# Layer 0 of a two-layer transformer: the FFN's, preparation's and output's matmuls queued behind the scores

## The chip, the cores and the metric

The kernel runs on one core of a Trainium2 chip. The metric is the device time of one launch in microseconds. Five engines with queues of their own work side by side: TensorE (matmuls and transposes, PE in the profile, its weight loads PEld), VectorE (DVE), ScalarE (ACT), GpSimd (POOL) and SyncE (SP, which here issues transfers).

## The reference, cut to what matters

Sixteen sequences of 512 tokens of width 128 run through two layers. The change touches layer 0 alone: half an FFN with FP4 quantization, attention with relative positions in keys and values, and half of the same FFN again.

```python
# layer 0, per sequence x [512, 128]; ln = layernorm without weights
def ffn(x):   # I = 352
    q = fp4_quant_dequant            # blocks of 16: scale = max|x|/6, values rounded to 8 steps
    h = silu(q(x) @ q(w_gate).T) * (q(x) @ q(w_up).T)
    return q(h) @ q(w_down).T
def attn(x):  # 16 heads of 8
    q, k, v = split(x @ W_qkv + b_qkv); q = q / sqrt(8)
    score = q k^T + q . rel_emb_k[clip(j - i, -64, 64) + 64]
    p = softmax(score)
    ctx = p v + p . rel_emb_v[clip(j - i, -64, 64) + 64]
    return ctx @ W_out + b_out
x = x + 0.5 * ffn(ln(x))
x = x + attn(ln(x))
x = x + 0.5 * ffn(ln(x))
# layer 1 follows (attention with experts, linear attention, attention with experts)
```

## The kernel before

The unit of work in layer 0 is half a sequence of queries (256 rows, all 16 heads); 32 units make the 16 sequences. Each is passed twice. `maxima` computes the scores of a unit in 32 blocks of 128 x 512 (`scores`, L263 and L267: four matmuls, and eight more where relative positions vary), reduces each on VectorE (L341), and from these gets the row maxima: two reductions (L347), a transpose on TensorE (L349), and transfers that put the negated maximum into the score operand as a bias row (L353, L355). `main` computes the 32 blocks again, now with the bias; ScalarE takes the exponential (L369), and the products with the values (`av`) and with the relative values (`rps`) follow in runs of 16 to 64 matmuls (`run`, L272 and L274). Score blocks of both passes share three PSUM buffers (`sps`, pool `pS`).

Around this run chains of smaller steps, written as Python generators that yield between steps:

- `head` and `tail`: `F.half`, half an FFN over 256 rows. Layernorm (L55 to L62), quantization (L70 to L81, the last two on GpSimd), transposes (L115) and a copy (L116), two times gate and up (L121 to L126), quantization, and for each of two halves transposes (L133), copies (L135, L136), three matmuls (L139) and the addition (L140). `head` works three sequences ahead; `tail` ends a unit and stores it.
- `prep` and `prepV`: layernorm, transposes (L282), Q and K (L286), splitting into two float16 parts and transfers to memory in another layout, products with the relative keys (L305); V (L319, L321). `prep` works two sequences ahead.
- `fin`: the output of the unit before. The addition of the relative part (L422), transposes (L430), the division by the softmax sums (L433, L434), transposes (L437), a copy (L438), the product with W_out (L440), additions (L442, L443).

All these matmuls write to two PSUM buffers (`mps`, pool `pM`).

A planner, `interleave`, decides in which order the code emits all this: each generator has a number of steps and a span of due times in units, and the generator whose next step is due first is called next. From the emitted order and from what depends on what, the language's scheduler makes each engine's final queue. It may issue an instruction ahead of ones emitted before it, where by its own account it is ready sooner. `tc.issue_after(ins)` is a means against this: what is traced inside it stands behind `ins` in the queue of `ins`'s engine; it adds an order and no wait. Before the change it is used for the runs of `av` and `rps` matmuls (L273) and for the addition of `fin` on VectorE (L425). Once in the queue, an engine's instructions start in order: one that waits holds up those behind it.

Before the loop stands a start: the first sequence's head, its preparation, its first maxima, the heads and preparation of the second sequence, 14 steps of the next maxima, the heads of the third.

Of the kernel before, what the change touches and what calls it, by code (L numbers as in the profile page):

```python
# [17 lines left out]
I = 352  # L18
# [7 lines left out]
class K:  # L26
# [23 lines left out]
    def ln_steps(s, xb, out, wk, n):  # L50

        nc=s.nc
        st=wk.tile([128,n,6],F32,name="ln_st"); mv=wk.tile([128,n,2],F32,name="ln_mv")
        for j in range(n):
            nc.vector.bn_stats(st[:,j,:],xb[:,j,:])  # L55
            nc.vector.bn_aggr(mv[:,j,:],st[:,j,:]); yield  # L56
        ve=wk.tile([128,n],F32,name="ln_ve"); rs=wk.tile([128,n],F32,name="ln_rs"); mr=wk.tile([128,n],F32,name="ln_mr")
        nc.vector.tensor_scalar(ve,mv[:,:,1],1e-5,None,ALU.add)  # L58
        nc.gpsimd.tensor_tensor(rs,ve,s.negh[:,:n],ALU.pow); yield  # L59
        nc.vector.scalar_tensor_tensor(mr,mv[:,:,0],-1.0,rs,ALU.mult,ALU.mult)  # L60
        for j in range(n):
            nc.scalar.activation(out[:,j,:],xb[:,j,:],AF.Identity,bias=mr[:,j:j+1],scale=rs[:,j:j+1])  # L62
        yield
    def quant_steps(s, X, wk, P, nb, tag):

        nc=s.nc
        n=nb*16
        X3=X.rearrange("p (b k) -> p b k",k=16)
        sc=wk.tile([128,nb],F32,name=tag+"_sc"); ri=wk.tile([128,nb],F32,name=tag+"_ri")
        nc.vector.tensor_reduce(sc[:P],X3,axis=AX.X,op=ALU.max,apply_absolute_value=True)  # L70
        nc.vector.tensor_scalar(sc[:P],sc[:P],float(np.float32(1/6)),1e-12,ALU.mult,ALU.max)
        nc.vector.reciprocal(ri[:P],sc[:P]); yield
        y=wk.tile([128,max(704,n)],F32,name=("q_y","q_yw")[n>704])[:,:n]; y3=y.rearrange("p (b k) -> p b k",k=16)
        nc.vector.tensor_tensor(y3[:P],X3,ri[:P].unsqueeze(2).to_broadcast([P,nb,16]),ALU.mult); yield
        M=wk.tile([128,max(704,n)],F32,name=("q_M","q_Mw")[n>704])[:,:n]
        nc.vector.tensor_scalar(M[:P].bitcast(U32),y[:P].bitcast(U32),0x7F800000,None,ALU.bitwise_and)
        nc.vector.tensor_scalar(M[:P],M[:P],1.0,C_MAG,ALU.max,ALU.mult); yield
        nc.vector.scalar_tensor_tensor(y[:P],y[:P],SHRINK,M[:P],ALU.mult,ALU.add); yield  # L78
        nc.gpsimd.tensor_tensor(M[:P],y[:P],M[:P],ALU.subtract)  # L79
        M3=M.rearrange("p (b k) -> p b k",k=16)  # L80
        nc.gpsimd.tensor_tensor(M3[:P],M3[:P],sc[:P].unsqueeze(2).to_broadcast([P,nb,16]),ALU.mult)  # L81
        yield M

class FFN:
# [22 lines left out]
    def half(f, xb, half, wk, pp):  # L107

        s=f.s; nc=s.nc
        xh=xb[:,2*half:2*half+2,:]  # L110
        xn=wk.tile([128,2,128],F32,name="f_x")
        yield from s.ln_steps(xh,xn,wk,2)
        for xq in s.quant_steps(xn.rearrange("p a b -> p (a b)"),wk,128,16,"xq"): yield
        ps=pp.tile([128,512],F32,name="mps")
        for j in range(2): nc.tensor.transpose(ps[:,j*128:(j+1)*128],xq[:,j*128:(j+1)*128],s.ident)  # L115
        xqT=wk.tile([128,256],F32,name="f_x"); nc.scalar.copy(xqT,ps[:,:256]); yield  # L116
        h=wk.tile([128,2,I],F32,name="f_h")
        for j in range(2):
            t=h[:,j,:]
            g=pp.tile([128,512],F32,name="mps")  # L120
            nc.tensor.matmul(g[:,:I],xqT[:,j*128:(j+1)*128],f.wguT[:,0,:],start=True,stop=True)  # L121
            nc.scalar.activation(t,g[:,:I],AF.Tanh,scale=0.5)
            nc.vector.scalar_tensor_tensor(t,t,1.0,g[:,:I],ALU.add,ALU.mult); yield
            u=pp.tile([128,512],F32,name="mps")
            nc.tensor.matmul(u[:,:I],xqT[:,j*128:(j+1)*128],f.wguT[:,1,:],start=True,stop=True)
            nc.vector.scalar_tensor_tensor(t,u[:,:I],0.5,t,ALU.mult,ALU.mult); yield  # L126
        for hq in s.quant_steps(h.rearrange("p a b -> p (a b)"),wk,128,44,"hq"): yield
        hq=hq.rearrange("p (a b) -> p a b",a=2)
        for j in range(2):
            ps=pp.tile([128,512],F32,name="mps")  # L130
            for c in range(3):
                P=min(128,I-c*128)
                nc.tensor.transpose(ps[:P,c*128:(c+1)*128],hq[:,j,c*128:c*128+P],s.ident)  # L133
            hT=wk.tile([128,3,128],F32,name="hT",bufs=1)
            nc.scalar.copy(hT[:,0:2,:],ps[:,:256])  # L135
            nc.scalar.copy(hT[:96,2,:],ps[:96,256:384])  # L136
            for c in range(3):
                P=min(128,I-c*128)
                nc.tensor.matmul(ps[:,384:512],hT[:P,c,:],f.wdT[:P,c,:],start=(c==0),stop=(c==2),skip_group_check=True)  # L139
            nc.vector.scalar_tensor_tensor(xh[:,j,:],ps[:,384:512],0.5,xh[:,j,:],ALU.mult,ALU.add); yield  # L140

def f16split(nc, src, hi, lo, eng_lo):
# [3 lines left out]
class Attn0:  # L146
# [110 lines left out]
    def scores(a, out, kt, half, b, BD, TQ, KS):  # L257

        nc=a.nc; blk=half*8+b
        sd=a.side(kt,blk); ib=a.inband(kt,blk)  # L260
        o4=out.rearrange("p (x g c) -> p g x c",x=8,g=4)
        for g in range(4):
            nc.tensor.matmul(o4[:,g],KS[:,sd,g*512+kt*128:g*512+(kt+1)*128],BD[:,g,:,b*32:b*32+32].rearrange("p h (x j) -> p x h j",j=4),start=(g==0),stop=(not ib and g==3),skip_group_check=True)  # L263
        if ib:
            for x in range(8):
                w0=kt*128-blk*32-x+a.OFF
                nc.tensor.matmul(out[:,x*64:x*64+64],a.ET[:,w0:w0+128],TQ[:,:,b*32+4*x:b*32+4*x+4],start=False,stop=(x==7),skip_group_check=True)  # L267

    xnT={}; pend={}; last=None
    def run(a, mms):  # L270
# [4 lines left out]
    def prep(a, b, xb, wk, pM):  # L275
# [3 lines left out]
        xn=wk.tile([128,4,128],F32,name="xn")  # L279
        yield from s.ln_steps(xb,xn,wk,4)  # L280
        ps=pM.tile([128,512],F32,name="mps")
        for j in range(4): nc.tensor.transpose(ps[:,j*128:(j+1)*128],xn[:,j,:],a.ident)  # L282
        xnT=a.xnT[b]=wk.tile([128,512],F32,name="xnT",bufs=2); nc.scalar.copy(xnT,ps); yield
        for z in range(2):
            ps=pM.tile([128,512],F32,name="mps")
            nc.tensor.matmul(ps,a.w[:,z*128:(z+1)*128],xnT,start=True,stop=True)  # L286
            f=wk.tile([128,512],F32,name="qk0") if z==0 else wk.tile([128,4,128],F32,name="xn").rearrange("p a b -> p (a b)")
            if z==0:
                for hf in range(2):
# [12 lines left out]
                nc.sync.dma_start((QS,KSd)[z][:,p*8:p*8+8,:],t)  # L302
            yield
        ps=pM.tile([128,512],F32,name="mps")
        nc.tensor.matmul(ps[:32],a.eb.rearrange("p a b -> p (a b)"),q,start=True,stop=True)  # L305
        rhi=wk.tile([128,512],F16,name="qkhi",bufs=2)[:32]; rlo=wk.tile([128,512],F16,name="qklo")[:32]
        nc.vector.tensor_copy(rhi,ps[:32]); nc.vector.tensor_tensor(rlo,ps[:32],rhi,ALU.subtract)
        for sd in range(2):
# [23 lines left out]
    def maxima(a, b, half, wk, pS, pM):  # L332
# [12 lines left out]
        mk=wk.tile([128,2,8,8],F32,name="mk")  # L345
        for hh in range(2):
            nc.vector.tensor_reduce(mk[:,hh],mx.rearrange("p k (x s) b -> p s b x k",s=2)[:,hh],axis=AX.X,op=ALU.max)  # L347
        ps=pS.tile([128,512],F32,name="sps")
        nc.tensor.transpose(ps[:,:128],mk.rearrange("p s b x -> p (s b x)"),a.ident)  # L349
        mt=wk.tile([128,32],F32,name="mt"); mn=wk.tile([128,32],F16,name="mn")  # L350
        nc.vector.tensor_reduce(mt,ps[:,:128].rearrange("p (c q) -> p q c",c=4),axis=AX.X,op=ALU.max)
        nc.vector.tensor_scalar(mn,mt,-1.0,None,ALU.mult)
# [63 lines left out]
    def fin(a, b, half, X, wk, pM):  # L416
# [10 lines left out]
        cn=wk.tile([128,2,128],F32,name="cn")  # L427
        for t in range(2):
            ps=pM.tile([128,512],F32,name="mps")
            for z in range(4): nc.tensor.transpose(ps[:,z*128:z*128+128],cx[:,z,t*128:t*128+128],a.ident)  # L430
            p3=ps.rearrange("p (h c) -> p h c",c=32)
            rc=wk.tile([128,16],F32,name="rc")
            nc.vector.reciprocal(rc,p3[:,:,8])  # L433
            nc.vector.tensor_tensor(cn[:,t,:].rearrange("p (h d) -> p h d",d=8),p3[:,:,0:8],rc.unsqueeze(2).to_broadcast([128,16,8]),ALU.mult)  # L434
            yield
        ps=pM.tile([128,512],F32,name="mps")
        for t in range(2): nc.tensor.transpose(ps[:,t*128:t*128+128],cn[:,t,:],a.ident)  # L437
        ct=wk.tile([128,2,128],F32,name="cn").rearrange("p a b -> p (a b)"); nc.scalar.copy(ct,ps[:,:256])  # L438
        ps=pM.tile([128,512],F32,name="mps")
        for t in range(2): nc.tensor.matmul(ps[:,t*128:(t+1)*128],ct[:,t*128:(t+1)*128],a.wo,start=True,stop=True)  # L440
        xh=xb[:,2*half:2*half+2,:]
        nc.gpsimd.tensor_tensor(xh,xh,a.bo.unsqueeze(1).to_broadcast([128,2,128]),ALU.add)  # L442
        nc.vector.tensor_tensor(xh,xh,ps[:,:256].rearrange("p (a b) -> p a b",a=2),ALU.add)  # L443
# [13 lines left out]
def layer0(tc, s, w, src, dst, nb=16):  # L457
# [3 lines left out]
    with ExitStack() as c:  # L461
# [53 lines left out]
            FFN1.pre(s,wp,[pA.tile([128,512],F32,name=f"av{z}") for z in range(2)]+[pA.tile([128,512],F32,name="rps")],w)  # L515
        big=c.enter_context(tc.tile_pool(name="big",bufs=3))
        loads(1); ffn2(head,1); run(prep(1)); run(part(14)); ffn2(head,2)
        S=[(part(99999),33*2*nb,W['part'],2*nb+W['part'])]
        for b in range(nb):
            for h in range(2):  # L520
                u=2*b+h
                def at(g,n,f,t): S.append((g,n,u+f,u+t))
                at(A.main(b,h,X,wk,big,pS,pA,pM),59,0,1)
                fn,tl=(W['fin'],W['tail']) if u<2*nb-2 else ((.3,.5),.6)
                at(A.fin(b,h,X,wk,pM),5,1+fn[0],1+fn[1])
                at(tail(b,h),21,1+fn[1]+.001,1+fn[1]+tl)
                if b+hl<nb: at(head(b+hl,h),21,*W['head'])
                if h==0 and b+pl<nb: at(prep(b+pl),11,*W['prep'])
                if h==1 and b+1<nb: at(prepV(b+1),1,*W['V'])
        interleave(*S)  # L530
# [507 lines left out]
```

## Time and profile before

| | |
|---|---|
| median of three runs | 3630.62 us (3627.19 to 3651.11) |
| the profiled execution | 3633.94 us |
| its span in the profile | 3632.2 us |
| TensorE busy in the span | 2825.0 us, 78% |
| VectorE busy | 2444.9 us, 67% |
| ScalarE busy | 1693.8 us, 47% |
| GpSimd busy | 838.9 us, 23% |
| granted TensorE clock, mean | 0.90 |
| layer 0's loop | from about 200 to 2000 us |

A busy time is the part of the span in which an engine worked, whatever the reason for the rest. A row of a group gives its line, engine, operation and tiles, the number of instructions, busy time and the mean of one in ns, and behind the bar the time that the engine sat idle just before such an instruction, with the instruction whose end released it. A row of the timeline gives start, duration and the same, with the idle time in square brackets. The rows that the prediction rests on stand there.

### The profile page before, as it was taken

The page shows a single profiled execution, that of the slowest core. Times are in us where ns is not written, and L with a number is a line of the kernel's source. Part 1 is how long each engine was busy: PE and PEld are TensorE (multiplying, and loading weights), DVE is VectorE, ACT ScalarE, POOL GpSimd, SP SyncE. Part 2 cuts the span into 40 slices and gives each one's busy share as a digit, 9 for nine tenths or more (in the row PEclk, how much of TensorE's full clock was granted, in tenths as well). Part 3 has the DMA queues.
Part 4 walks back from the last instruction along what each step waited for, and adds up shares of the span by engine and source line. Part 5 has one row for each costly group of instructions (what it writes and reads, how often), then busy time and mean ns, then how long its engine had stood idle before and what let it go on. Part 6 is the DMA issues. An engine that isn't in the chain of part 4 may idle for free. (4 is left out here: it accounts for less than half of the span.)

```text
span 3632.2 us, 95259 instructions
## 1 busy us (share of the span) xinstructions
PE 2825.0 (78%) x40077; PEld 2032.3 (56%) x40077; DVE 2444.9 (67%) x6508; ACT 1693.8 (47%) x3391; POOL 838.9 (23%) x789
## 2 busy tenths in 40 slices
PE   5578989889898889888896388873788888878570
PEld 3357777667676677666775244431565555555230
DVE  5568788777887788877773467774546655655356
ACT  3145555545455454545554155533455454445242
POOL 4122222222222222222110222212112211111226
PEclk8799999999999999999998599886899989989785
DMA  3232222321223222222210111104312222121401
GB/s 105 54 91 71 57 53 59 81 63 52 65 65 77 64 50 58 76 74 62 53 33 19 32 33 36 36 33 123 90 54 73 59 63 56 36 62 36 126 17 46
DMA packets 290159, 217.23 MB, mean 60 GB/s; under 512 B 77402, under 2 KB 257476, under 8 KB 289604
## 3 DMA queue, kind: packets, MB, share of 16 engines
q1 hardware_dynamic: 284468, 207.72, 21.6%
q8 instruction: 315, 5.16, 0.6%
q10 hardware_dynamic: 5264, 3.43, 0.4%
q14 instruction: 112, 0.92, 0.1%
HBM read 110.28 MB, written 100.78 MB: 58 GB/s over the span
## 5 line engine op out<-in xcount | busy, mean ns | idle before, releaser
L341 DVE TRANSPOSE_TENSOR_REDUCE mx<-sps 128x16 f32<-128x512 f32 x1024 | 702.5, 701 | 261.7 <-PE sps L263 137.2
L263 PE MATMUL sps<-a_BD,a_KS 128*128 128x128 f16 x8192 | 736.4, 222 | 136.2 <-DVE mx L341 65.6
L369 ACT ACTIVATE PT<-sps 128x512 f32<-128x512 f32 x1024 | 576.4, 599 | 433.8 <-PE sps L267 238.1
L263 PEld LDWEIGHTS <-a_KS 128*128 128x128 f16 x8192 | 546.1, 98 | 296.4 <-issue 260.0
L59 POOL TENSOR_TENSOR ln_rs<-ln_ve,negh 128x4 f32<-128x4 f32 (+1 forms) x192 | 176.9, 930 | 855.1 <-DVE ln_ve L58 760.6
L267 PE MATMUL sps<-a_TQ,a_ET 128*128 128x64 f16 x7168 | 370.3, 195 | 0.0
L721 DVE SCALAR_TENSOR_TENSOR moe<-mps,oh,moe 128x128 f32<-128x128 f32 x896 | 289.8, 341 | 110.7 <-PE mps L719 96.5
L79 POOL TENSOR_TENSOR q_M<-q_y,q_M 128x704 f32<-128x704 f32 (+2 forms) x129 | 157.0, 1218 | 784.6 <-DVE q_y L78 658.6
L719 PE MATMUL mps<-f_W,T 128*128 128x512 f32 x512 | 297.1, 701 | 24.8 <-DVE moe L721 20.0
L267 PEld LDWEIGHTS <-a_ET 128*128 128x128 f16 x7168 | 311.2, 99 | 2.3 <-issue 1.9
L274 PE MATMUL av<-PT,a_V 128*32 128x256 f32 x3840 | 251.9, 387 | 0.0
L894 DVE TENSOR_TENSOR a_at<-pp,a_cm 128x1024 f32<-128x1024 f32 x128 | 154.3, 1214 | 79.6 <-PE pp L892 78.6
L892 PE MATMUL pp<-a_F 64*128 64x128 f32 x2048 | 169.8, 306 | 41.4 <-DVE a_at L894 30.2
L892 PEld LDWEIGHTS pp<-a_F 64*128 64x128 f32 x2048 | 143.3, 206 | 93.0 <-DVE a_at L894 36.9
L719 PEld LDWEIGHTS mps<-f_W,T 128*128 128x128 f32 x512 | 102.7, 222 | 125.0 <-issue 75.3
L274 PEld LDWEIGHTS av<-PT,a_V 128*32 128x32 f32 x3840 | 121.4, 111 | 68.7 <-issue 5.0
L874 ACT ACTIVATE a_F<-pp 128x1024 f32<-128x1024 f32 x128 | 127.0, 1025 | 46.8 <-PE pp L872 40.5
L62 ACT ACTIVATE xn<-xn,ln_mr,ln_rs 128x128 f32<-128x128 f32 x256 | 103.6, 481 | 95.5 <-DVE ln_mr L60 75.2
L274 PE MATMUL rps<-PT,a_TV 128*32 128x64 f32 x6912 | 134.5, 222 | 4.6 <-issue 4.4
L139 PE MATMUL mps<-wdT,hT 128*128 128x128 f32 (+1 forms) x768 | 126.9, 301 | 5.6 <-ACT hT L136 4.0
L673 ACT COPY f_PT<-St 32x512 f32<-32x512 f32 x128 | 78.7, 615 | 106.0 <-DVE St L672 99.9
L872 PE MATMUL pp<-a_QK,a_PK 128*128 128x512 f16 x256 | 82.7, 413 | 54.4 <-DMA a_QK<-a1d 26.6
(342 smaller groups left out, 5330.2 us busy)
## 6 DMA issues: line engine op xcount, KB each, us to landing
QM<-a_HM SPq DMA_DIRECT2D x180, 128.0 KB
a_TQ<-QM SPq DMA_DIRECT2D x120, 192.0 KB
RD<-RV SPq DMA_DIRECT2D x32, 512.0 KB
a_KS<-KSd SPq DMA_DIRECT2D x128, 96.0 KB
a_QK<-a1d SPq DMA_DIRECT2D x128, 96.0 KB
xn<-X SPq DMA_DIRECT2D x32, 256.0 KB
a1d<-a_hi SPq DMA_DIRECT2D x64, 128.0 KB
a_BD<-QS SPq DMA_DIRECT2D x128, 58.0 KB
```

What stands on the lines that cost most here:

```text
L59: nc.gpsimd.tensor_tensor(rs,ve,s.negh[:,:n],ALU.pow); yield
L79: nc.gpsimd.tensor_tensor(M[:P],y[:P],M[:P],ALU.subtract)
L263: nc.tensor.matmul(o4[:,g],KS[:,sd,g*512+kt*128:g*512+(kt+1)*128],BD[:,g,:,b*32:b*32+32].rearrange("p h (x j) -> p x h j",j=4),start=(g==0 ...
L267: nc.tensor.matmul(out[:,x*64:x*64+64],a.ET[:,w0:w0+128],TQ[:,:,b*32+4*x:b*32+4*x+4],start=False,stop=(x==7),skip_group_check=True)
L274: for p,q in mms[1:]: a.nc.tensor.matmul(*p,**q)
L341: with a.s.tc.high_priority(): r=nc.vector.tensor_reduce(mx[:,kt,:,bb],ps.rearrange("p (i c) -> p i c",c=32),axis=AX.X,op=ALU.max,apply_tr ...
L369: nc.scalar.activation(pt[:,:,bb*32:bb*32+32].rearrange("p h (x j) -> p x h j",j=4),ps.rearrange("p (x h j) -> p x h j",x=8,j=4),AF.Exp)
L719: nc.tensor.matmul(ps,yT[:,j*128:(j+1)*128],a.W[:,e2*4:e2*4+4,:],start=True,stop=True)
L721: nc.vector.scalar_tensor_tensor(moe[:,j,:],ps[:,e*128:(e+1)*128],oh[:,j,e2*4+e:e2*4+e+1],moe[:,j,:],ALU.mult,ALU.add)
L874: nc.scalar.activation(f,ps,AF.Relu)
L892: nc.tensor.matmul(ps[:,hh,bs],f[hh*64:hh*64+64,1,bs],f[hh*64:hh*64+64,0,bs],start=True,stop=True)
L894: nc.vector.tensor_tensor(k,ps.rearrange("p h (b q) -> p (h b) q",b=4),a.cm.unsqueeze(1).to_broadcast([128,8,128]),ALU.mult)
```

## The change

Each score block now records its last matmul (`lastmm`), whichever pass it belongs to. A new `gate` puts what is traced inside it behind that matmul in TensorE's queue. It is laid around all matmuls and transposes of `F.half`, of `prep`, of `fin`, and around the transpose of the maxima; `prepV` (L319) is left as it is. Before the first score block there is nothing to stand behind, and the gate does nothing. Three chains get one step more: `F.half` yields between the copies and the last matmuls (twice, once for each half), `maxima` ahead of its transpose, `fin` between its copy and the product with W_out. The planner's step counts follow: 21 to 23, 33 to 34, 5 to 6, with the same due times.

```diff
+    lastmm=None
+    def gate(s):
+        return s.tc.issue_after(s.lastmm) if s.lastmm is not None else ExitStack()
...
 # F.half
-        for j in range(2): nc.tensor.transpose(ps[:,j*128:(j+1)*128],xq[:,j*128:(j+1)*128],s.ident)
+        with s.gate():
+            for j in range(2): nc.tensor.transpose(ps[:,j*128:(j+1)*128],xq[:,j*128:(j+1)*128],s.ident)
...
-            nc.tensor.matmul(g[:,:I],xqT[:,j*128:(j+1)*128],f.wguT[:,0,:],start=True,stop=True)
+            with s.gate(): nc.tensor.matmul(g[:,:I],xqT[:,j*128:(j+1)*128],f.wguT[:,0,:],start=True,stop=True)
...
+            with s.gate():
+                for c in range(3):
+                    P=min(128,I-c*128)
+                    nc.tensor.transpose(ps[:P,c*128:(c+1)*128],hq[:,j,c*128:c*128+P],s.ident)
+            hT=wk.tile([128,3,128],F32,name="hT",bufs=1)
+            nc.scalar.copy(hT[:,0:2,:],ps[:,:256])
+            nc.scalar.copy(hT[:96,2,:],ps[:96,256:384]); yield
             for c in range(3):
                 P=min(128,I-c*128)
...
-                nc.tensor.matmul(ps[:,384:512],hT[:P,c,:],f.wdT[:P,c,:],start=(c==0),stop=(c==2),skip_group_check=True)
+                with s.gate(): nc.tensor.matmul(ps[:,384:512],hT[:P,c,:],f.wdT[:P,c,:],start=(c==0),stop=(c==2),skip_group_check=True)
...
 # scores
+        a.s.lastmm=getattr(r,"ins",r)
...
 # prep: the same gate around L282, L286, L305
 # maxima
+        yield
         ps=pS.tile([128,512],F32,name="sps")
-        nc.tensor.transpose(ps[:,:128],mk.rearrange("p s b x -> p (s b x)"),a.ident)
+        with a.s.gate(): nc.tensor.transpose(ps[:,:128],mk.rearrange("p s b x -> p (s b x)"),a.ident)
...
 # fin: the gate around L430 too
         ps=pM.tile([128,512],F32,name="mps")
-        for t in range(2): nc.tensor.transpose(ps[:,t*128:t*128+128],cn[:,t,:],a.ident)
-        ct=wk.tile([128,2,128],F32,name="cn").rearrange("p a b -> p (a b)"); nc.scalar.copy(ct,ps[:,:256])
+        with s.gate():
+            for t in range(2): nc.tensor.transpose(ps[:,t*128:t*128+128],cn[:,t,:],a.ident)
+        ct=wk.tile([128,2,128],F32,name="cn").rearrange("p a b -> p (a b)"); nc.scalar.copy(ct,ps[:,:256]); yield
         ps=pM.tile([128,512],F32,name="mps")
-        for t in range(2): nc.tensor.matmul(ps[:,t*128:(t+1)*128],ct[:,t*128:(t+1)*128],a.wo,start=True,stop=True)
+        with s.gate():
+            for t in range(2): nc.tensor.matmul(ps[:,t*128:(t+1)*128],ct[:,t*128:(t+1)*128],a.wo,start=True,stop=True)
...
 # layer0: the step counts
-        S=[(part(99999),33*2*nb,W['part'],2*nb+W['part'])]
+        S=[(part(99999),34*2*nb,W['part'],2*nb+W['part'])]
...
-                at(A.fin(b,h,X,wk,pM),5,1+fn[0],1+fn[1])
-                at(tail(b,h),21,1+fn[1]+.001,1+fn[1]+tl)
-                if b+hl<nb: at(head(b+hl,h),21,*W['head'])
+                at(A.fin(b,h,X,wk,pM),6,1+fn[0],1+fn[1])
+                at(tail(b,h),23,1+fn[1]+.001,1+fn[1]+tl)
+                if b+hl<nb: at(head(b+hl,h),23,*W['head'])
```

More of the change, by code (lines that the diff above doesn't have):

```diff
@@ L124, in half @@
             u=pp.tile([128,512],F32,name="mps")
-            nc.tensor.matmul(u[:,:I],xqT[:,j*128:(j+1)*128],f.wguT[:,1,:],start=True,stop=True)
+            with s.gate(): nc.tensor.matmul(u[:,:I],xqT[:,j*128:(j+1)*128],f.wguT[:,1,:],start=True,stop=True)
             nc.vector.scalar_tensor_tensor(t,u[:,:I],0.5,t,ALU.mult,ALU.mult); yield
@@ L130, in half @@
             ps=pp.tile([128,512],F32,name="mps")
+            with s.gate():
[5 more added lines that the diff above has]
+            nc.scalar.copy(hT[:96,2,:],ps[:96,256:384]); yield
             for c in range(3):
                 P=min(128,I-c*128)
[L133 to L138, printed above, removed]
-                nc.tensor.matmul(ps[:,384:512],hT[:P,c,:],f.wdT[:P,c,:],start=(c==0),stop=(c==2),skip_group_check=True)
+                with s.gate(): nc.tensor.matmul(ps[:,384:512],hT[:P,c,:],f.wdT[:P,c,:],start=(c==0),stop=(c==2),skip_group_check=True)
             nc.vector.scalar_tensor_tensor(xh[:,j,:],ps[:,384:512],0.5,xh[:,j,:],ALU.mult,ALU.add); yield
@@ L262, in scores @@
         for g in range(4):
-            nc.tensor.matmul(o4[:,g],KS[:,sd,g*512+kt*128:g*512+(kt+1)*128],BD[:,g,:,b*32:b*32+32].rearrange("p h (x j) -> p x h j",j=4),start=(g==0),stop=(not ib and g==3),skip_group_check=True)
+            r=nc.tensor.matmul(o4[:,g],KS[:,sd,g*512+kt*128:g*512+(kt+1)*128],BD[:,g,:,b*32:b*32+32].rearrange("p h (x j) -> p x h j",j=4),start=(g==0),stop=(not ib and g==3),skip_group_check=True)
         if ib:
@@ L266, in scores @@
                 w0=kt*128-blk*32-x+a.OFF
-                nc.tensor.matmul(out[:,x*64:x*64+64],a.ET[:,w0:w0+128],TQ[:,:,b*32+4*x:b*32+4*x+4],start=False,stop=(x==7),skip_group_check=True)
+                r=nc.tensor.matmul(out[:,x*64:x*64+64],a.ET[:,w0:w0+128],TQ[:,:,b*32+4*x:b*32+4*x+4],start=False,stop=(x==7),skip_group_check=True)
+        a.s.lastmm=getattr(r,"ins",r)
     xnT={}; pend={}; last=None
@@ L281, in prep @@
         ps=pM.tile([128,512],F32,name="mps")
-        for j in range(4): nc.tensor.transpose(ps[:,j*128:(j+1)*128],xn[:,j,:],a.ident)
+        with s.gate():
+            for j in range(4): nc.tensor.transpose(ps[:,j*128:(j+1)*128],xn[:,j,:],a.ident)
         xnT=a.xnT[b]=wk.tile([128,512],F32,name="xnT",bufs=2); nc.scalar.copy(xnT,ps); yield
@@ L285, in prep @@
             ps=pM.tile([128,512],F32,name="mps")
-            nc.tensor.matmul(ps,a.w[:,z*128:(z+1)*128],xnT,start=True,stop=True)
+            with s.gate(): nc.tensor.matmul(ps,a.w[:,z*128:(z+1)*128],xnT,start=True,stop=True)
             f=wk.tile([128,512],F32,name="qk0") if z==0 else wk.tile([128,4,128],F32,name="xn").rearrange("p a b -> p (a b)")
@@ L304, in prep @@
         ps=pM.tile([128,512],F32,name="mps")
-        nc.tensor.matmul(ps[:32],a.eb.rearrange("p a b -> p (a b)"),q,start=True,stop=True)
+        with s.gate(): nc.tensor.matmul(ps[:32],a.eb.rearrange("p a b -> p (a b)"),q,start=True,stop=True)
         rhi=wk.tile([128,512],F16,name="qkhi",bufs=2)[:32]; rlo=wk.tile([128,512],F16,name="qklo")[:32]
@@ L429, in fin @@
             ps=pM.tile([128,512],F32,name="mps")
-            for z in range(4): nc.tensor.transpose(ps[:,z*128:z*128+128],cx[:,z,t*128:t*128+128],a.ident)
+            with s.gate():
+                for z in range(4): nc.tensor.transpose(ps[:,z*128:z*128+128],cx[:,z,t*128:t*128+128],a.ident)
             p3=ps.rearrange("p (h c) -> p h c",c=32)
@@ L436, in fin @@
         ps=pM.tile([128,512],F32,name="mps")
-        for t in range(2): nc.tensor.transpose(ps[:,t*128:t*128+128],cn[:,t,:],a.ident)
-        ct=wk.tile([128,2,128],F32,name="cn").rearrange("p a b -> p (a b)"); nc.scalar.copy(ct,ps[:,:256])
+        with s.gate():
+            for t in range(2): nc.tensor.transpose(ps[:,t*128:t*128+128],cn[:,t,:],a.ident)
+        ct=wk.tile([128,2,128],F32,name="cn").rearrange("p a b -> p (a b)"); nc.scalar.copy(ct,ps[:,:256]); yield
         ps=pM.tile([128,512],F32,name="mps")
-        for t in range(2): nc.tensor.matmul(ps[:,t*128:(t+1)*128],ct[:,t*128:(t+1)*128],a.wo,start=True,stop=True)
+        with s.gate():
+            for t in range(2): nc.tensor.matmul(ps[:,t*128:(t+1)*128],ct[:,t*128:(t+1)*128],a.wo,start=True,stop=True)
         xh=xb[:,2*half:2*half+2,:]
```

## The prediction

> **What bounds the kernel now.** I read the page first, then the busy table of layer 0's loop (200 to 2000 us), then TensorE's groups and the time they sat idle there, then timelines of single stalls.
>
> ```profile
> PE 2825.0 (78%) x40077; PEld 2032.3 (56%) x40077; DVE 2444.9 (67%) x6508; ACT 1693.8 (47%) x3391; POOL 838.9 (23%) x789
> ```
> ```profile
> 200.00:2000.00 1800.00, 1567.82 (x28188) 1236.60 (x28179) 1369.82 (x3029) 904.40 (x1983) 394.52 (x369) 0.97 0.24 60
> ```
>
> The first line is the page's. The second is the loop alone (busy us of TensorE, its weight loads, VectorE, ScalarE, GpSimd; granted clock; transfers' share): TensorE is busy 1567.8 of 1800 us (87%), VectorE 76%, ScalarE 50%, at a granted clock of 0.97. TensorE is the bound, with 232 us of idle time in it. Its groups say what that time stands in front of:
>
> ```profile
> L263 PE MATMUL sps<-a_BD,a_KS 128*128 128x128 f16 x7900 | 706.7, 222 | 108.3 <-DVE mx L341 58.1 <-ACT PT L369 35.1 <-issue 2.9
> ...
> L121 PE MATMUL mps<-wguT,f_x 128*128 128x352 f32 x230 | 92.5, 484 | 4.8 <-DVE f_h L126 4.5 <-DVE f_h L123 0.4
> ...
> L133 PE MATMUL mps<-ident,q_M 128*128 128x128 f32 x348 | 56.8, 285 | 6.5 <-POOL q_M L81 5.4 <-issue 0.5 <-DVE x L443 0.2
> L430 PE MATMUL mps<-ident,cx 128*128 128x128 f32 x248 | 40.4, 288 | 18.7 <-DVE cx L422 12.5 <-DVE f_h L126 6.1
> ...
> L440 PE MATMUL mps<-a_wo,cn 128*128 128x128 f32 x124 | 22.6, 306 | 13.5 <-ACT cn L438 11.4 <-issue 2.1
> ...
> L437 PE MATMUL mps<-ident,cn 128*128 128x128 f32 x62 | 19.0, 308 | 22.0 <-DVE a_V L321 19.8 <-DVE qklo L307 2.2
> ...
> L349 PE MATMUL sps<-ident,mk 128*128 128x128 f32 x31 | 9.7, 314 | 21.9 <-DVE mk L347 12.0 <-DVE hq_sc L71 9.9
> ```
>
> About half, 108.3 us, is in front of score matmuls (L263) that wait for one of three score buffers, which VectorE (L341) or ScalarE (L369) still reads. The other half is in front of matmuls of the FFN, the preparation and the output: over all lines that the change queues anew it is 98.6 us. Two places show what such a wait does to the rest:
>
> ```profile
> 856.37 0.62 PE L263 MATMUL sps<-a_BD,a_KS 128*128 128x128 f16 x8
> ...
> 857.58 1.01 DVE L321 TENSOR_TENSOR a_V<-mps,a_bev 128x384 f32<-128x384 f32 x2
> ...
> 858.73 0.30 PE L437 MATMUL mps<-ident,cn 128*128 128x128 f32 x1 [1.75 <-DVE a_V L321]
> ...
> 861.19 0.37 ACT L438 COPY cn<-mps 128x256 f32<-128x256 f32 x1 [3.58 <-PE mps L437]
> ```
> ```profile
> 1949.26 1.12 PE L430 MATMUL mps<-ident,cx 128*128 128x128 f32 x4 [9.87 <-DVE cx L422]
> ```
>
> In the first, the transposes of the output (L437) stand at the head of TensorE's queue until VectorE has read a buffer of the same pool (L321); no score runs behind them, and ScalarE is idle 3.58 us. In the second, the last but one output holds TensorE 9.87 us while the last half's scores stand behind it.
>
> **The change part by part.** *The order.* The due times in the planner fix the order in which the code emits. I laid that order beside the trace's order on TensorE, occurrence by occurrence of each line. Of the newly gated matmuls 68% stand today ahead of score blocks emitted before them: those of L115 mostly by 10 to 12 blocks, L437 in 39 of 64 cases (24 by 12 blocks), L430 by 3 on average, L349 never. A score block takes 0.4 to 0.8 us in the timelines, so 12 are 5 to 10 us. All of these move back behind those blocks; their inputs, made by VectorE, ScalarE and GpSimd, do not move, so they should lie ready. The idle time divides in the same count: 47.7 us before matmuls that stand ahead (all 22.0 of L437, 13.0 of L430, the 4.8 of L121 nearly whole, 4.8 of L305, the rest small) and 50.9 before matmuls that don't.
>
> Term 1: of the 47.7 I take 40. Ends: 0, if the waits are for buffers that are late 10 us later too, and 47.7. Nearest row: L437's wait of 1.75 us for L321, which starts 1.15 us before the wait ends and is long done 12 blocks on.
>
> *The added steps.* A step between the copy at L438 and the product at L440: its 13.5 us are before matmuls that today follow straight on. Where L437 now comes 12 blocks later the product does too; in the halves where the chain runs late nothing changes: 7 of 13.5 (ends 0 and 13.5). A step before the transposes of the maxima (L349): one step of the maxima is a 34th of a unit of 58 us (L349 comes at 861.6, 919.2 and 977.6), 1.7 us, in which the planner emits about one score block of the main pass. The mean wait is 21.9/31 = 0.71 us, one block 0.4 to 0.8: 14 of 21.9 (ends 0 and 21.9). The step between the copies at L135/L136 and L139 finds only 3.4 us of waits: 0 (ends 0 and 3.4; and a loss, since the buffer of L133 is now held a 23rd of a unit, 2.5 us, longer, four times a unit, 10 of the 116 buffer-us that two buffers have in 58 us).
> What these steps carry along: behind the maxima's step go L351, L352 and six transfers on SyncE's queue (L353, L355), 1.7 us later; the bias rows they bring are used when the next half begins, some 30 us on (L349 at 861.6, the half's end at 893.6), and the loop shows 0.3 us of waits for them. L442 and L443 shift by under 1 us. The steps' counts grow within the same due times, so chains end where they ended.
>
> Together: 40 + 7 + 14 = 61 us of waits removed.
>
> *What is late next.* TensorE reaches the following scores earlier, with three buffers as before. Of 1975 score blocks (7900/4) 153 waited for VectorE or ScalarE, 8%, 0.61 us each. A block reached 0.7 us earlier will wait more often; I take a quarter of the 61 as given back, 15 us. Ends: none, and all 61. VectorE's 24% idle time, over half of it spent waiting for scores (134.2 + 104.2 us), speaks for the lower part.
>
> *The start.* There the gate holds the first FFN halves and the second preparation behind all 32 blocks of the first maxima:
>
> ```profile
> 125.33 0.58 PE L263 MATMUL sps<-a_BD,a_KS 128*128 128x128 f16 x4 [17.14 <-DMA a_BD<-QS]
> 126.15 1.04 PE L263 MATMUL sps<-a_BD,a_KS 128*128 128x128 f16 x8
> 126.99 1.48 PE L121 MATMUL mps<-wguT,f_x 128*128 128x352 f32 x2
> ...
> 163.37 0.30 PE L349 MATMUL sps<-ident,mk 128*128 128x128 f32 x1 [0.91 <-DVE ln_mv L56]
> ```
> ```profile
> 91.00:125.30 34.30, 3.13 (x6) 1.38 (x7) 2.34 (x5) 0.84 (x2) 1.15 (x1) 0.52 0.56 125
> 125.30:163.70 38.40, 28.26 (x287) 22.93 (x288) 36.03 (x79) 5.55 (x16) 9.68 (x8) 0.76 0.02 7
> ```
>
> From 91 to 125 the scores wait for transfers, and TensorE does only 3.1 us of FFN in the gap, which is lost. From 125 to 164 VectorE is full (36.0 of 38.4). Alone, 32 reductions of 0.70 us would end at 125.3 + 22.4 = 147.7, so the first maxima can end up to 15.7 us sooner. Against it the first gated half, done by 164, starts only then, and the second preparation (at 171 to 179) with it: up to 20 us later, and with it the scores of the second batch. I take 0 between -15.7 and +20.
>
> [...]
>
> **Sum.** 61 removed, 15 given back, 0 at the start: -46. The profiled execution took 3633.9 us (its span 3632.2), which makes 3588. It lies 3.3 us above the median of the runs, 3630.6; against that median 3588 is 1.2% less. About 1% (36 us) is what a measurement of this kernel can tell from no change.
>
> **Rivals.**
> *The gap filler is lost (slower).* Today a ready FFN matmul slips in where scores can't go. The gated groups hold 510 us of busy time without L349, 68% of it ahead of its scores: 345. Each tenth of it that filled a gap which now stays empty costs 35 us. At three tenths: +104 - 46, 3692; it decides from 13% on. For it: the 93 us of waits for buffers at L263 are gaps that nothing filled. Against it: greedy filling uses up the fillers early, and the waits come where none are left.
> *All is given back (no change).* The 61 us turn into waits at L263, because VectorE is what stretches the crowded parts: 3634. For it: VectorE works through the whole stall at 856 to 862.
> *Evener flow (faster still).* Spreading the FFN matmuls also halves the 93 us of waits for score buffers: 61 + 46, 3527. For it: the waits bunch where VectorE is crowded, while elsewhere it idles.
> *The gate doesn't bind.* If the scheduler's order already obeyed it, 3634; the count above, 68% ahead, speaks against it.
>
> **How the numbers follow.** The forecast (own range 3555 to 3615) 40%, the lost filler 23%, all given back 22%, evener flow 10%, not binding 5%; nearly all of the forecast and all of evener flow are faster by over 1% (0.47), the lost filler and a little of the neutral cases slower by over 1% (0.26), the rest 0.27. The range, 3525 to 3685, reaches into the lost filler up to some 28% of it unfilled (about 0.1 lies beyond) and to evener flow whole (0.05 beyond).
>
> **What would show it.** Right: L437 and L430 with less than a third of their 22.0 and 18.7 us, the 9.87 us wait gone, L349 near 8 us, L440 near 6, and L263 at 110 to 130 us of idle time in the loop. Wrong: L263 over 170 us (filler lost, or all given back: then the loop's length decides between them), the second batch's first scores waiting for a_BD by over 10 us, or gated waits that stay near 98 us.

## The result, and the profile after

The changed kernel takes 3888.81 us in the median (3880.76 to 3901.86), the kernel before 3632.09 on the same chip: a ratio of 1.07 (95% interval 1.0651 to 1.0749), some 257 us slower. The profiled execution took 3885.51 us, its span is 3883.8, 251.6 more than before. Layer 0's loop is longer by nearly all of it:

```profile
200.00:2220.00 2020.00, 1570.19 (x27940) 1234.97 (x27938) 1375.87 (x3017) 909.20 (x1971) 398.73 (x371) 0.92 0.21 55
```

TensorE's work is the same (1570 us of busy time against 1568), spread over 220 us more, at a granted clock of 0.92 where it was 0.97. Its groups in the loop (L269 is the L263 of before, L441 is L430, L449 is L437, L453 is L440, L359 is L349):

```profile
L269 PE MATMUL sps<-a_BD,a_KS 128*128 128x128 f16 x7848 | 706.0, 221 | 381.7 <-DVE mx L350 142.0 <-DVE ln_mv L56 139.9 <-DVE ln_mr L60 40.3
...
L441 PE MATMUL mps<-ident,cx 128*128 128x128 f32 x248 | 39.5, 283 | 2.7 <-DVE f_h L128 2.3 <-DVE f_h L131 0.4
...
L453 PE MATMUL mps<-a_wo,cn 128*128 128x128 f32 x124 | 24.9, 331 | 0.4 <-DVE qklo L316 0.4
...
L449 PE MATMUL mps<-ident,cn 128*128 128x128 f32 x62 | 13.6, 291 | 0.0
...
L359 PE MATMUL sps<-ident,mk 128*128 128x128 f32 x30 | 9.5, 318 | 11.2 <-DVE mk L356 11.2
```

Most of the waits that the change was to take away are gone: over all gated lines 98.6 us became 40.1. But the idle time in front of the scores rose from 108.3 to 381.7 us, and its new releasers are layernorm's instructions on VectorE (L56, L60), which have nothing to do with score buffers. VectorE's own list of waits says why (us in total, times, the longest; before, then after):

```profile
DVE ln_st L55 <- DMA x<-in_L_attn_x_dram: 45.5, 11, 5.2
```
```profile
DVE ln_st L55 <- DMA x<-in_L_attn_x_dram: 218.5, 11, 20.7
```

Eleven times, once for each sequence whose x is loaded in the loop, VectorE stands some 20 us at the first instruction of the next head (L55), which reads x before it has landed; it was 4 us before. One of them, on VectorE and on TensorE:

```profile
1121.97 0.25 DVE L146 SCALAR_TENSOR_TENSOR x<-mps,x 128x128 f32<-128x128 f32 x1
1123.60 0.29 DVE L146 SCALAR_TENSOR_TENSOR x<-mps,x 128x128 f32<-128x128 f32 x1 [1.38 <-PE mps L145]
...
1145.50 0.87 DVE L55 BATCH_NORM_STATS2 ln_st<-x 128x6 f32<-128x128 f32 x4 [19.22 <-DMA x<-in_L_attn_x_dram]
```
```profile
1127.75 0.39 PE L269 MATMUL sps<-a_BD,a_KS 128*128 128x128 f16 x4
1147.18 0.59 PE L269 MATMUL sps<-a_BD,a_KS 128*128 128x128 f16 x4 [19.05 <-DVE ln_mv L56]
```

At 1122.2 the tail has made its last addition to the x whose buffer is to be loaded again (the addition at 1123.60 belongs to a head, whose result is normalized right after it). VectorE can read the new x 23 us later. VectorE's reductions stand behind L55, the three score buffers fill, and TensorE stops for 19 us; ahead of the stall four matmuls took 0.39 us, behind it 0.59. Where the 23 us go is seen on SyncE, which issues the store of the old x and the load of the new one (`X<-x`, `x<-in_...`), first after:

```profile
1110.81 3.42 SPq L324 DMA_DIRECT2D a_KS<-KSd  x6
...
1125.65 3.38 SPq L339 DMA_DIRECT2D a_TQ<-QM  x1
1129.13 0.72 SPq L416 DMA_DIRECT2D RD<-RV  x1
1138.57 1.36 SPq L419 DMA_DIRECT2D a_cr<-RD  x4
1140.03 0.39 SPq L499 DMA_DIRECT2D X<-x  x1
1142.54 0.39 SPq L488 DMA_DIRECT2D x<-in_L_attn_x_dram  x1
```

and before:

```profile
988.23 0.88 SPq L315 DMA_DIRECT2D a_KS<-KSd  x2
989.21 0.39 SPq L486 DMA_DIRECT2D X<-x  x1
992.14 0.39 SPq L475 DMA_DIRECT2D x<-in_L_attn_x_dram  x1
992.63 1.67 SPq L315 DMA_DIRECT2D a_KS<-KSd  x4
994.35 0.26 SPq L329 DMA_DIRECT2D a_BD<-QS  x1
```
```profile
988.86 0.29 DVE L140 SCALAR_TENSOR_TENSOR x<-mps,x 128x128 f32<-128x128 f32 x1 [1.32 <-PE mps L139]
...
997.09 1.07 DVE L55 BATCH_NORM_STATS2 ln_st<-x 128x6 f32<-128x128 f32 x5 [4.40 <-DMA x<-in_L_attn_x_dram]
```

Before, the pair stood in the middle of the next unit's operand loads, and the load went out 3 to 5 us after the last addition. After, the pair stands behind all of them, behind the store of the relative part (RD<-RV), and behind the transfers that read it back and wait until it has landed (a_cr<-RD, 9 us here); the load goes out 20 us after the last addition. The tail's end has moved as well: counted from the issue of the maxima's result (MD) the last addition came 8 us later before and 19 us after (medians over the eleven loads), some 11 us more. That the later tail cost the pair its place is argued, not shown. SyncE's order comes from the scheduler and not from the tail's end in the run, and in e2 below the loads stand 10 to 20 us behind the last addition although the tail ends only 9 us after the same issue.

### The profile page after: what moved, and what is told of

Same layout as the page of the kernel before. It is cut to its first block, busy times and chain, and to the rows that moved or that the text cites. A ratio compares the mean times of both kernels' runs of the same rounds, so it can differ in the third digit from the quotient of the medians.

```text
span 3883.8 us, 95177 instructions
## 1 busy us (share of the span) xinstructions
PE 2835.7 (73%) x40077; PEld 2033.6 (52%) x40077; DVE 2456.2 (63%) x6508; ACT 1705.0 (44%) x3391; POOL 841.1 (22%) x789
## 5 line engine op out<-in xcount | busy, mean ns | idle before, releaser
L269 PE MATMUL sps<-a_BD,a_KS 128*128 128x128 f16 x8192 | 738.4, 221 | 425.6 <-DVE mx L350 149.6
L269 PEld LDWEIGHTS <-a_KS 128*128 128x128 f16 x8192 | 548.4, 98 | 578.7 <-issue 543.6
L59 POOL TENSOR_TENSOR ln_rs<-ln_ve,negh 128x4 f32<-128x4 f32 (+1 forms) x192 | 174.9, 920 | 782.8 <-DVE ln_ve L58 665.8
L282 PE MATMUL av<-PT,a_V 128*32 128x256 f32 x3840 | 263.7, 401 | 0.0
L55 DVE BATCH_NORM_STATS2 ln_st<-x 128x6 f32<-128x128 f32 x192 | 45.9, 266 | 218.8 <-DMA x<-in_L_attn_x_dram 218.5
```

What stands on the lines that cost most here:

```text
L269: r=nc.tensor.matmul(o4[:,g],KS[:,sd,g*512+kt*128:g*512+(kt+1)*128],BD[:,g,:,b*32:b*32+32].rearrange("p h (x j) -> p x h j",j=4),start=(g= ...
L282: for p,q in mms[1:]: a.nc.tensor.matmul(*p,**q)
```

## The experiments

The ratios, with their 95% intervals, are to the kernel before on the same chip (single runs of it took 3616 to 3657 us over all chips). The chips differ by some 20 us, so differences between times of different chips are good to that. Theory A: the reload of x. Theory B: withheld matmuls that used to fill gaps. Theory C: a tail that is late whatever the queue.

**e1 and e2: x in halves.** Both kernels; the loads by halves, ten buffers of 256 rows.
```diff
-xk bufs=5;  t=xk.tile([128,4,128]);  xload(b)
+xk bufs=10; t=xk.tile([128,2,128]) per half;  xload(b,(h,))
```


> The changed kernel with each sequence's x held in two tiles of 256 rows (ten in place of five of 512, the same memory), each loaded when its own half of the head begins; nothing else. The first half's load then no longer needs the last tail to be stored. Theory A (the 252 us come from the reload of x: its store and load fall behind other transfers in SyncE's queue, and VectorE stands some 20 us per sequence at L55 with everything behind it): VectorE's wait for x falls from 218 us to under 40, TensorE's idle time before L269 in the loop from 382 to under 200, the time to 3600 to 3690. Theory B (matmuls that filled gaps are withheld, so gaps stay empty everywhere; the wait at L55 only is where the slack collects): the wait at L55 falls too, other waits take its place, and the time stays above 3830.

> The same two-tile x in the kernel before. A: its 45 us of waits for x at L55 vanish, the time falls by 10 to 50 us, to 3580 to 3620. B: nothing to gain there, 3632 within 10.


Measured: 4073.97 us (ratio 1.124, 1.1216 to 1.1264) and 3900.01 (1.0763, 1.0731 to 1.0795). Both forecasts of A missed by hundreds of us, the other way. B's time for e1, above 3830, came true, but the wait did not fall, and e2 refutes B's 3632. The waits at L55 doubled in number: 22 with 398 us in e1, 22 with 285 us in e2:

```profile
DVE ln_st L55 <- DMA x<-in_L_attn_x_dram: 285.3, 22, 17.8
```

In e1 every load went out right behind a store, some 20 us after the last addition; in e2 the loads went out 10 to 20 us after it, every other one behind the transfers into a_TQ. So the kernel before falls into the same stall when its transfers change places, without any gate. A was wrong in where it put the wait (the last tail's data) and not refuted in what it costs.

**e3 and e4: the change in two.** Gate without the added steps; steps without the gate.
```diff
 e3: without the three added yields, counts 21, 33, 5
 e4: -return s.tc.issue_after(s.lastmm) if s.lastmm is not None else ExitStack()
     +return ExitStack()
```


> The gates alone, without the added steps and with the old step counts. If the gate is what makes the tail late (A and B both): 3830 to 3900. If the added steps do it: under 3700.

> The added steps and new counts alone, gate off. If the gate is the cause: 3632 within 30, VectorE's wait for x near 45 us. If the steps make the tail late: above 3750, with a wait for x above 150 us.


Measured: 3862.61 (1.0657, 1.0634 to 1.0679), wait at L55 202 us; 3841.79 (1.0601, 1.0569 to 1.0632), wait 218 us. Each part alone costs nearly the whole. Their losses don't add. In both traces the load stands behind the wait for RD, as after the whole change, 20 us behind the tail's last addition, so the loss can fall only once, a reading that no run tests.

**e5 to e8: the pair on GpSimd's queue.** In the changed kernel, the kernel before, the gate alone, the steps alone.
```diff
-nc.sync.dma_start(t,tok(src,b))  ;  nc.sync.dma_start(tok(dst,b)[...],X[b][...])
+nc.gpsimd.dma_start(t,tok(src,b));  nc.gpsimd.dma_start(tok(dst,b)[...],X[b][...])
```


> The changed kernel with the store of x at the end of a tail and the load of the next x issued on GpSimd's queue in place of SyncE's. Theory A (the store and the load stand on SyncE's queue behind a unit's operand transfers and behind the transfer that waits for RD, some 15 us): the load now goes out within 6 us of the last addition to x, VectorE's wait at L55 falls from 218 to under 90 us, and the time to 3600 to 3720. Theory C (the tail itself ends too late, whatever queue): the wait stays above 150 us, the time above 3800. Theory B (withheld matmuls cost TensorE everywhere): the wait falls, the time stays above 3800.

> The same move of the two transfers in the kernel before. A: there they were hardly held up (the load 3 to 5 us behind the last addition), so 3623 within 40. B and C expect the same here; it is the base for the run of the changed kernel.

> The gates without the added steps, the two transfers on GpSimd's queue. A: the wait at L55 under 90 us, 3600 to 3700. B: above 3800, since the gate is what withholds matmuls.

> The added steps without the gates, the two transfers on GpSimd's queue. A: the wait at L55 under 90 us, 3600 to 3700. C: unchanged near 3840.


Measured: 3824.48 (1.0497, 1.0462 to 1.0532), 3701.10 (1.0158, 1.0123 to 1.0192), 3768.47 (1.0341, 1.0311 to 1.0371), 3718.59 (1.0213, 1.0177 to 1.025). In e5 the load goes out 7 us after the last addition, not 20, and the wait at L55 falls from 218 to 55 us: C's forecast is refuted. But A's times were missed in all four, and e5 by itself came out as B had said: the wait falls, the time stays above 3800. Part of that is the move's own price, 57 us in e6. There VectorE's waits for x grew from 45 to 70 us, and GpSimd waited 68 us in front of the stores with its quantization behind them. Such a wait in e5:

```profile
1088.45 0.75 POOL L499 DMA_DIRECT2D X<-x  x1 [12.17 <-DVE x L146]
```

Against e6 the change still costs 123 us, half of what it was; e7 67, e8 17. These runs don't decide between A and B.

**e9 to e11: the first read moved, the transfers left on SyncE.** The load is emitted where it was; the head's steps begin later, and L55 stands on VectorE behind the last reduction emitted so far. In the changed kernel, the kernel before, the gate alone.
```diff
-if b+hl<nb: at(head(b+hl,h),23,*W['head'])
+if b+hl<nb:
+    if h==0: at(xl(b+hl),1,-.1,0)        # xl: xload(b) and one yield
+    at(head(b+hl,h),23,.35,1.05)
 # ln_steps, for heads of reloaded x
-nc.vector.bn_stats(...); nc.vector.bn_aggr(...); yield
+with s.tc.issue_after(s.lastred): nc.vector.bn_stats(...); nc.vector.bn_aggr(...)
+yield
```


> The changed kernel with the load of x where it was, but the head's steps starting 0.45 of a unit later in the planner, and its reads of x at L55 queued on VectorE behind the last reduction of a score block emitted so far: 14 reductions stand between the last addition to the old x and the first read of the new one, where there were 2 or 3. All transfers stay on SyncE. Theory A (VectorE's queue held at its head by a load that goes out some 18 us late): the wait falls from 218 to under 60 us, the time to 3620 to 3760. Theory B (withheld matmuls): the time stays above 3800, whatever becomes of the wait.

> The same in the kernel before (15 reductions between, where there were 2). A: its 45 us of waits for x go, 3580 to 3635. If the later, denser heads cost something by themselves: 3640 to 3720, and the run of the changed kernel is to be compared with that.

> The gates without the added steps, with the later first read (12 reductions between). If the gate by itself costs what GpSimd's queue showed (67 us more than its base): 50 to 90 us above the same edit of the kernel before. If that cost came from GpSimd's queue: within 25 us of it.


Measured: 3660.95 (1.0043, 1.0028 to 1.0058), 3603.62 (0.9884, 0.9866 to 0.9903), 3640.07 (0.9997, 0.9984 to 1.0011). The wait for x falls to 10 us in e9 and to 2 in e10; e11 keeps 48.

```profile
DVE ln_st L59 <- DMA x<-in_L_attn_x_dram: 9.6, 7, 4.0
```

The changed kernel gets 228 us faster by an edit that leaves every gate and every added step in place, and the same edit makes the kernel before 39 us faster: the change's price falls from 257 to 57 us. A holds, and B, which had the time above 3800 here, is out as the main cause. The edit does two things at once, the later steps of the head (its matmuls too are emitted later) and the read's place in VectorE's queue; no run separates them. e11 is 36 us above e10, between its two forecasts. e10 is faster than both kernels, although its load now goes out nearly as late as after the change:

```profile
990.35 0.71 SPq L411 DMA_DIRECT2D RD<-RV  x1
991.16 0.79 SPq L493 DMA_DIRECT2D X<-x  x1
...
1000.92 0.39 SPq L480 DMA_DIRECT2D x<-in_L_attn_x_dram  x1
```
```profile
982.29 0.28 DVE L145 SCALAR_TENSOR_TENSOR x<-mps,x 128x128 f32<-128x128 f32 x1
...
1005.56 0.25 DVE L59 BATCH_NORM_STATS2 ln_st<-x 128x6 f32<-128x128 f32 x1
```

The load goes out 18 us behind the last addition, and L59 (the L55 of before) starts with no idle time in front of it. A late load costs VectorE nothing here; what it waited for after the change was a read queued too early, in front of everything else.

**e12: the start without the gate.**
```diff
+gated=False until interleave(*S); gate only if s.gated
```


> The changed kernel with the gate off until the loop begins. The start's part of the loss is read from the time of the fourth transpose of the maxima (338.5 before, 355.6 after): this run should have it near 340, and a total of 3870, 17 us below the changed kernel; unchanged at 3889 if the start's delay is made good later.


Measured: 3869.75 (1.0622, 1.0606 to 1.0637), 19 us below the changed kernel, as expected; the fourth transpose of the maxima begins at 334.8. The two times are from different chips: each against the kernel before on its own, the difference is 29 us.

**e13 to e18: what the gate is worth by itself.** All with the later first read: e13 the gate in the loop alone; e14 the whole change with the gate in the loop alone; e15 the steps; e16 the gate around the output's matmuls; e17 and e18 are e13 and e16 with the heads' steps at .45 to 1.1.
```diff
 e13, e14: e12's edit      e16: gate() around L430, L437, L440 only
 e17, e18: -at(head(b+hl,h),21,.35,1.05)
           +at(head(b+hl,h),21,.45,1.1)
```


> The gates without the added steps, off until the loop begins, with the later first read of x. Between 3604 (the kernel before with the later read) and 3640 (the gates from the start on). If the loop gains what was forecast for it (46 us): under 3590. If the start alone makes the gates dear: 3600 to 3625. If the gate costs in the loop too: 3625 to 3645.

> The whole change, gate off until the loop begins, with the later first read of x. The whole change with the later read took 3661; the start was worth 19 us, so 3642 within 10. If the loop gains: under 3604.

> The added steps without the gates, with the later first read. They alone cost 219 us without it. Theory A: nearly all of that goes, 3604 to 3640. If the steps do harm of their own: above 3660.

> The gate around the output's matmuls alone (L430, L437, L440 of the kernel before), no added step, with the later first read. The forecast saw its largest waits there, 54 us in all, of which 9.9 at the end of the loop. If they are worth taking away: under 3590. If they only turn into waits of the scores: 3604 within 10.

> As the gates in the loop with the later first read, the head's steps another tenth of a unit later, so that 14 reductions and not 12 stand before the first read of x. That run still had 49 us of waits for x. If these are what kept it at 3625: the waits fall under 20 us and the time to 3585 to 3605. If the gate costs by itself: 3615 to 3630.

> As the gate around the output alone with the later first read, the head's steps another tenth of a unit later. That run had 42 us of waits for x. If these hid a gain: 3575 to 3600. If the output's waits only turn into waits of the scores: 3604 to 3616.


Measured: 3625.02 (0.9949, 0.9932 to 0.9966), 3639.88 (0.9991, 0.9975 to 1.0007), 3669.00 (1.0073, 1.0048 to 1.0097), 3615.40 (0.9924, 0.9897 to 0.995), 3654.99 (1.0032, 1.0014 to 1.005), 3642.33 (1.0009, 0.9987 to 1.0031). None comes below e10's 3604, so nothing of the forecast gain shows; e16 lies just above the range for waits that only turn into waits of the scores. Up to the loop's last score, the idle time in front of gated lines is 60 us in e13 against e10's 72, in front of scores 123 against 114, in front of the av and rps runs 28 against 16: 12 us removed, some 20 come back. The balance is less than half of the 21 us between the two times; the rest isn't explained. e15 missed: the steps alone still cost 65 us against e10, more than with the gates in the loop (e14, 36). e17 and e18 missed as well: the waits for x went, as expected, but the times rose by 30 and 27 us; their transposes of the maxima waited 38 and 37 us where e13 and e16 had 22 and 20, and the rest of the rise isn't explained.

## Why the prediction was wrong

*The order and the waits removed: right.* The gate did bind. 61 us of waits were to go, and 58.5 went: L437 from 22.0 to 0.0, L430 from 18.7 to 2.7 with its wait of 9.87 us, L440 from 13.5 to 0.4 (7 were claimed), L349 from 21.9 to 11.2 (14 were claimed).

*The step that failed: "the steps' counts grow within the same due times, so chains end where they ended".* The planner's due times held, but the tail's last addition came some 11 us later (9 with the gates alone, e3, and 6.5 with the added steps alone, e4), and the load into its buffer went out 20 us behind that addition where it had been 3 to 5. The prediction followed the transfers of the maxima's step and not those behind the tail, the store and the reload of x, nor the VectorE instruction that waits for them. The list of VectorE's waits had it, 45.5 us in 11 pieces, the largest wait there for a transfer; it was read for the scores' share alone. As a term: wait for x forecast at no change, measured +173 us. With it out of the way the change's price falls from 257 to 57 us (e9 against e10), so the stall and what follows it carry about 200. How the pair lost its place on SyncE stays open.

*"What is late next": mis-sized.* 15 us were to come back in front of the scores; 273 did, most of them for the reload. Without the reload's stall more came back than went (e13: some 20 for 12).

*The start.* The first maxima did end 15 us sooner, their transpose at 148.1 for 163.4, as the lower bound had it. But the second batch's first scores waited for a_BD, one of the prediction's own signs of being wrong (before, then after):

```profile
PE sps L263 <- DMA a_BD<-QS: 2.1, 1, 2.1
```
```profile
PE sps L269 <- DMA a_BD<-QS: 12.5, 1, 12.5
```

The fourth transpose came at 355.6 for 338.5. The chosen value of 0 was some 17 to 21 us by the traces and 19 or 29 by the times (e12), near its upper bound of 20 or above it.

*The clock.* The forecast's sum has no term for it, and the loop's granted clock fell from 0.97 to 0.92. Around the stall shown it was 1.00 ahead (1110 to 1127), 0.54 over the stall itself (1128.2 to 1147.2) and 0.50 for 3 us behind it, where four matmuls took 0.59 us for 0.39. Behind all eleven stalls it was 0.50 for 3 to 6 us, 48 us together. If TensorE's work went at half speed in that time, 24 us of the 257 lie there, an estimate from these figures; no run shows that share by itself.

*The rivals.* The slower rival ended on the right side by the wrong mechanism, and its own sign, L263 over 170 us, came up for another reason. No run shows that a lost filler was the cause: e9 keeps the same gates and is 228 us faster. Whether one has a part in the 57 us that remain isn't tested. "All is given back" fits what the gate does once the reload is set apart; why e15, e17 and e18 are slower than that stays open.

## What to carry to other kernels

An edit that shifts a chain shifts the transfers at its end, so follow the chain to the buffer it frees, to the load into it, and to the first instruction that reads it: that instruction's place in its engine's queue decided here whether a late load cost nothing (e10) or 20 us a time. The waits of 4 us at the head of VectorE's queue were the warning, since little separated the read from the load (2 reductions); 15 reductions put between them, with the head's steps later, were worth 1.2%, and a load that goes out 18 us late no longer held VectorE. An edit whose two halves each cost nearly the whole can be one cliff and not two prices.

## What the runs showed of the hardware

SyncE's queue was a resource of its own here. In the stretch shown after the change, one transfer into a_TQ (192 KB) held it for 3.38 us; over the loop before, such transfers took 0.3 to 3.7 us of it. And a transfer that waited for another to land held all behind it, 9 us at L419. The transfer engines were busy for only 0.21 of the loop after the change, but the place in the queue was worth more than the time of issuing. The stores and reloads of x take 22 us of SyncE over the loop after the change, and moving them to GpSimd made the changed kernel 64 us faster (76 when each is counted against the kernel before on its own chip) and the kernel before 57 us slower.
